# Another order of issue and other places in memory for a four-layer kernel

## The chip, the cores and the metric

The kernel runs on one core of a Trainium2 chip. A core has a matmul engine (TensorE, PE in the profile), a vector engine (VectorE, DVE), an activation engine (ScalarE, ACT), a general one (GpSimd, POOL) and a sync engine (SyncE, SP) that here only issues DMAs. Each engine works off its own queue of instructions in order, and waits at an instruction until what it needs is there. Operands lie in SBUF, an on-chip memory of 128 partitions; products go to PSUM, which has eight banks of 128 x 512 floats here. The metric is the device time of the core in microseconds (us), the median over runs; beside it there is one profiled execution with a record of every instruction.

## The reference: what is computed

Two sequences (batches) of 1024 tokens with 128 channels pass through four layers. Each layer has the same frame, and its own pair of blocks:

```python
xn = layernorm(x)
s = attn_i(xn)
g = silu(ffn_i(xn))
x = x + s * g
```

- Layer 0, attention: q, k and v by projections, causal convolutions of four taps and silu; a delta rule in chunks of 32 tokens with four heads of 32 channels. In each chunk a 32 x 32 triangular system is inverted, row by row; then a state S goes from chunk to chunk:

```python
u_i = ui - wi @ S
o_i = qi @ S + mask(qi @ ki.T) @ u_i
S = S + ki.T @ u_i
```

  Its output is mixed with v and with two longer convolutions of v (7 and 25 taps) by a small router, that takes the input and the means, variances and mean products of the four branches (56 features), has one hidden layer and ends in a softmax. Layer 0, feed-forward: four wide products of 512 hidden channels with gates and gelu, and a narrow one back to 128.
- Layer 1: softmax attention of 16 heads over all 1024 tokens, with a distance-like score; a mixture of eight experts, two for each token.
- Layer 2: linear attention of 16 heads; a block that only the 127 tokens of highest score go through, with attention among these.
- Layer 3: causal attention with 16 query heads and one key head; two blocks of local attention in windows of 64 tokens with rotary positions.

All arithmetic is in 32-bit floats.

## The kernel before

**Two passes.** `program` (L2270) doesn't issue instructions. It runs over layers, batches and blocks and calls the engines through stand-ins (`Engines`, L629), and a `Record` (L493) notes each call as a unit. A unit is one instruction, or on PE a run of up to 32 matmuls of the same shape in the array that follow one another in the same block and batch (`note`, L520; `product`, L548). For each unit it is worked out from the regions of the buffers which earlier units must come first. There are 7120 units. The costs and lags given in the engines' stand-ins are noted, but at issue nothing is decided by them.

**The order** is a table. `ORDER` (L297) is a packed string; `Record.order` (L568) unpacks it into the numbers of all units in the order in which they are issued, with one more bit per unit. A copy out of PSUM that may be done by either of two engines (`evac`, L723) goes to DVE where the bit is set, and else to ACT. There are 480 such copies. Since the blocks of both batches are all in one list, the order also says how they interleave: the recurrence of batch 1 runs among the work of batch 0 for layer 0, and so on.

**The places** are a table too. Tiles come from pools: 35 large ones of 128 x 1048 floats (`half`), 21 of 128 x 512 (`t512`), 14 small ones, eight PSUM banks, and a few more. `PLACES` (L424) gives for each buffer, when its first use is issued, which slot of its pool it takes, 4594 in all. A slot's next buffer can't be written before the last use of the one before.

`Record.issue` (L584) then walks through the order, draws places and issues all instructions from L604; so each row of the profile carries this line, and what an instruction belongs to is read from its operands' names. DMAs are units as well: loads of weights and input are issued by SP, the experts' gathers by POOL.

**Layer 0**, on which much of the following turns, has these steps for each batch (`l0_attn`, L813). The input x is normalised to `xn` (ACT and DVE), transposed on PE (`tr`, with an identity matrix that lies in the first part of `const`) and copied to `xnT`. PE projects it (`proj`, with weights `w_a`), the result is copied to `pad`, and DVE convolves it (`acc`). Norms follow (`ss`), products of keys (`kk`), the triangular systems (`nn`), which go through a scratch memory to another layout (`scr_n`, `ncol`), where a loop of products and sums on DVE inverts them (`prod`, `u`), and back by eight DMAs (`scr_u`, `td`). Then tiny products of 32 x 32 blocks on PE: `pu` (twelve groups of 32, between them copies and subtractions on the way to `uw` and `vk`), `chunk` and `au`, from which DVE makes `step`, `add` and `read`. The recurrence is thirty times the same pair:

```python
C.mm(ps[r, :DH], at(step, c)[r], at(state, c)[r], tile_position=(32 * h, 32 * h))
nc.vector.tensor_tensor(at(state, c + 1), ps[:, :DH], at(add, c), ALU.add)
```

Four matmuls into `next` on PE, one addition into `state` on DVE, each waiting for the other. The convolutions of 7 and 25 taps (`conv`) are 32 DVE instructions over 1024 elements each. Features (`feat`) are transposed to `fT`; the router's hidden layer is `rh`, its output `logit`, its softmax starts with `lg`. The feed-forward block (`l0_ffn`, L1173) has the products `p`, `ph` and `w` on PE (`w` is the narrow one; a group of it is called w3 below), with weights `w_f_0` to `w_f_5`. Layer 1's attention begins with the scores `sim`, then `e` (the exponential on ACT) and `av`.

Of the kernel before, what the change touches and what calls it, by code (L numbers as in the profile page):

```python
# [20 lines left out]
AF = mybir.ActivationFunctionType  # L21
ALU = mybir.AluOpType
X = mybir.AxisListType.X
PSUM = bass.MemoryType.PSUM

P = 128
NB = 2
L = 1024
T = NB * L
NT = T // P  # L30
TB = L // P
# [225 lines left out]
def pack_inputs(inputs):  # L257
# [29 lines left out]
PE, ACT, DVE, POOL, SP = range(5)  # L287
# [10 lines left out]
    "c-mcg2VfLc*Y=#5*^*5sjZ_E;9i(>*L_nJKj#5+<QC@m8o86gBHWX2mA|SkA0TED8I!F^~p$Q@-w2%e~q>!H7o!z<Lxpx+P|9>~xow;+%xu-nm"  # L298
    "Id{K%mk%P9XUU9Vb~SUtly9dFezOLk-u~ACKu`rkT|z-X(3y6m@^L~G|3e>uD1d`Q4i-;`!i!={;aI=hxkDQ69lUNL_TN3|Zy2P9k_!(;HCgd?"
    "<ny26JBL-f{7iM=<JP+XzHoMMkNtTR6n)d`uGOcav}qOa{LXPdz55_KEPsueEStW6UWMN8{{GPkS*_|8uC9g%H+aM%Fg<|wPeUpTIy`;>&{%gD"  # L300
    "60#dVgqTvl2oaZ^wgs-jlO_fI;MHp<1Ppq0b8G;9==O~`r*CK2JEW6AA&npT#PLeunIxql<i;1c60;M&ouBbLe3bz3wc)pM-Qu<xbjudr{J2}d"
    "2=eHkxgWuv7k>IJxl2~0x^-2*zW)LYuDqL5QkzVvGX+!yl=ym_`h@xORB#(eG|c<*ad~(Q{PP+>K`hLl69<J+Wg#d-?yliYEgwh0d*8xiXLGn)"
    "9;{zpZ<=T0SMQ|h;s8Ef4og;Gw;6h6!~Ld_C;JwD^v#4bg%I(4{;DAdBc8t{ck=G2YRs|s_Wa&eyD5pyM^i;ArGqaIuDr<S!Q@>rm3{>gd>06+"
    "46OV$s_SK_D4%)oS6K7C)am1WPovikjeSODH~)Cxi28bmF!blG@1Jq<t4G96Sosn7C{uUTnO4QKsUIwK9D8GPVqaso%fd<lzP(X5we4<c$ib06"
    "6<wG(a`?Vg^IOfF@yi(K^e%ji-B-YmLnDm8z+07jl@AZU`#|vH;PHtMb-s!qE?dO&KB9SHw1Ft5hq0n*>Q-lINrLWSGh#4*RAqE~+^^LY=C^(_"
    "PTd_GeXcRz`<#F3?1-$Y57xpb1CI^*k7E0)<28UmuJc>IA01^)HI{}k>;Hc**#;;3;`jbx07szwV{{mwA3EOUxBBc-q072}wdJn-$Ro68g-ZAX"
    "+n1dY>W$p9a`i{|p=RcH{l~ori4S!z>TQn6I0F?TxPx6T_r)YXSFJz%cgLY&aB7Wy8q@{^uK4cK!7r4f0lnc=pG(0_9ScYNvMA^CMZI7=EH$6r"
    "r8rD4qCQ)dE5zOo+_m5ubST8Qq3-apSv7^u{R*Ji;fa490T6ROZEIj<PCQI~c66%L2<|llV`L8ev)exE@^7C*t|23+#rd89cPe+Rz1sqv0m6l%"
    "F~86q%v$@=E>cks;Ap3z2ZmZYV^d}~rUf4We*4>RZfM*Eek7Ay3k6?I3N1bA@R{-W7}QSRKHPshfN8`}q0OQW_YdAt7&38Ne#hqlRRf>?GvJso"
    ">i7PKl&pmZOCrQd5nnuH&Ddz(0|LPP;&7NH9yl+bc;j@B3jno)Z(Qgx{c7$0x4!w$opa6p=wiZ!HACQ6dzb&^jWYz@u2C1BjXXS9cMRLQ>vSyu"  # L310
    "R&Tp@H1<(kyVW}P>|1vh<ii@Ze8{;uUw40drlA&unb$7}A8wp6rv?Av`cGhe+>pi5dI*>Z8{0!?xZP@76?{Cs?Z=xc7qXRpD{;m^IV||^^J!N*"
    "Ke#je=$pbZo(woVkl)5bQNyobZk;CvDvVX4UsPdDWHtph@Ez51iNBCDYwy$6d9ekBUGgFJ39%0iX<h!#QMlXmZd0d8aR*mG*t7aj?g^_g)v0{T"
    "st54q&k+##La0~k3?xONpu4*OPL+)N^BDw*FAPSVtM5URLm+|WLNFo3DJt=KpeCsKx2{wBPj!?Xf4ew#Uwvq41h-D$d5_L%<ONj`6qCSv+=3CE"
    "67>wV{!S3}YMsBr_snzzD27_yr6iZmr~C(a@4_EtA!RL$<AV9=uy$S3{-iGW(4cjbF7!Vf(Sqy)80HCj;lEUR5@Hh63&&Cg0})k^52-amtVkZ6"
    "nq+Vng$oA7?U$XvD{6IwaxC)fS(rTJdK++=iXucpbSj8~>H#Bh3*xuJqLt&PZxIFe<*pu4AVc6F1Xh2%=|mEU#8eaT&JWJx@Rnk5ebJ_u|Dj}G"
    "hdbC4pUo>iCWq3iiw!-&q?QG!;boqPLSLt->IHBa+=^u`1P0U@Krwi*i>L~8+xR53^p*dxFT;JurVn_xF7UHYmoI|y5WziJ(JMPE;oUtvFOWIw"
    "#JP6k!d-0+EwCHvz~tk^pf!{SK&8P4YJ6M;(E{-SN0eAJ=GUx=H-?{v7reW;c@+`dsQ#P;GWfwmk9q=z#TAGiw_6|gM8AFp@u1EeHCy3lxa4Vj"
    "o97*8d;2?8|KElM&z|S!ERKZunvIWV92@O~pFVl<?E3JA()(nW&xEML+AXo=lU9$ssOuzbSh{LaRX`|Q+45eXP<&xT!L8QUNBA6Xyxy>GNqBYr"
    "*0*;0d^g^MX!1j7am}h_y>2u+Gv?qJfS-4MI(9i9SWQUN(9E_F+vn6_pAU8y^gF?S^GWen?+?BOpC3LQ*Yfw&3tjC7*Vii+%_itN;<}Fo-c%5F"
    "bK0A7i(k9Pk6+}5`O#amvd7eB1($R1ciX?)1U3A7!p{}Sov*BJy>6{DSa^5qUtEX4-@;qpU%Jn8EwSI#7kwZpcI23!biOP8S(no+2R>gDb1M72"  # L320
    "KRRC9lyRCrJ|H>d-Iz2|Ij=#bW3hUr^V$_9K1T-=P*rE*lx@YKe97#^ZJrB@KNrt-zu4UqQc<rwI43qQp~}aI!Jrq_^3Y0OLtR9tAgA#;c)$QP"
    "5Vw8OkNqJCj`DfY@wug9^Be7Sx4@%wd#Xd*hMw%Fh$CT8LwBbeuZ5rMpLgk6pT>{)H;#*Zx!(8LU;UF8PtA>Qc0V`n(7+Qz;c-3qI%OGv`9Z?+"
    "rg6}E)glqr&2g?UFO}L4H?Ntq6wJypSn4qG<XXEWymWV$U0GdeldWJ{vT_k`^+~V$Y_VOq>h9q%iF21__E@~qz&mtvR&AMP0A2w-U*ihUdBk_W"
    "uMMg7==@ZNfp@ue#v0M%8`*jIKJHZ(ax~Z3m*~<0${G|zLai^)lPA#FLHz2ToS2>s8#7X~_GdMAY?~6i^22v_cygf~%eVKyF*@lue3-KAj+C~o"
    "fA4_;5dtcLNo5f5Rl(){4pSxeGU*&XzIBB6D+^V4QWpfzLaSaE&ihoo4(AbgLZBsF@*(wweE$W?x5f3<O1{pdl)elreEBJ1B_7!MRo<6V129#L"
    "?Ai;uor8ugclWP-QBP3o-+_9f!$)-bT<i{>BNIgxj<z@W9}ySAdH3%FK^4LTC<-eHE8YKE!foVZ7oNiiFjo5W^<MDgR#JJO)91Gl6{mN7>(U9z"
    "!I51Tj}|&ya@QV&$+ueZ;O2#MNxbn`GI1LeW8$L*c@4H2x_Jx$p1n`fUO0RMx58Y=&1&XZo;YUJl*Gm2&u_0=Qvr{+*6Oo^EA%%H#>RHMW*lBr"
    "9V%G66;8b}=qUJzoy!N#8!KLj{a%Q@*b}0RPU9afgJUoBKGPOAkvV_#I|+535870GkiVflxz%?eT+Z!UH1GSr8pc7x*k}<NJ+^;dk(|4BX3m03"
    "FK!>4xTaxjVw}IQanGss^EbSGd+j%Y`3LeIZ1eo{T1M3PT^)Q|JHRI$W&zav)TN!_613%}yiqs$_LbC2@o!E0U}?WL8Fwr$bH#oq9KHR{iYY@J"
    "74<EdEn1chSik08y#9XEmHA+Xz?}6BVR2F9O$hofsCL#Ps6IX`aK&3NY0}s|ec{&f22qLI8!RP}3$O1B^5egLZ>Ft2{PIWZ83k{jb$0^4v+d*Z"  # L330
    "|H^B9tG+(aeqx(Xm-@$s^i55;1f%oesxT5B>n}{+M`{9&t?haS3NCepe}?U-3n@z`X9j1!_BRiv+e0A`&a@5szF}JsZWXr)`hD=ph&v6%@?N%;"
    "-K;^L$02^BbvK~xUET5SOZ$cub?@`lJG+FpVoSmrTuTr2gHmIcTdi-6^7*k<r)A6Dn2>O*>a^u%RrP15JhzPlzOl=_T3`Ls$GWyj2e>lu*nKFR"
    "SA4Q>GsCKd$Nz>lJ&wWy0UEve4NN~@D^HnN8+q(;qk*2Yj*dTcxSh}uxz-1RM||SsPZ*)c$-Ylb{SUeBJ{kZYo;cS0;M=3kJx}#{TIqjiz{BV!"
    "uz5(m^PR6Zf^5ugx?2xNJ<vyHZJ6EWXJO#&M~N+cuD$UmG<bBcnFzN%)3?ImCG}4<T05^Be`f9CX)t@xf~C*kpEE0#%=~Jp!83P2ygz)lrr(+X"
    "n7Zzp!Z4kCG0ZRNUNrmrIk2%tuOB-*)Vg(kd2o4PLXXR?*VleO^}pr22kswsr1LuY@{!J=jY4fgtLR4U^J*N~2_cbl6W)39<Fd_nrk%bty2bC8"
    "S7&dp*Q62}Gz44snO6gDwLadYYRq51wCGq_S^m6Xa6Q=8JvV>!(^#KR-)s|7{ZDoGi}&AB5_3Fvd~06|ygJ~>{g4L1&DMW%vDBykt<ds<qKd>?"
    "MHIS*?(AOgwap379hJ|Ux4Q8FIzIhqc}qui4%CZMdS1TS&ebBv@8B9pi}JZ?&)YJ1cnPd7Y&CXu+2f%_4;wvRFAr`rH$1HLEBR_d=Udn2!`jW;"
    "9z5>cpdkF<qWy`jPX}i<;U7ibHP!bk4vsAl2QL^)?p6ffiZAln2Xim#Eo#=|ORM1T`2L#?)&2O+kC5SZExoa`Lrc+~(tJw0d(({%AN4%sd#YP$"
    "K<CEJl&(*LrtnR!?eQJs+|YPX-QnEu$(_fUrrf`=5GI|w2ZkzRS(nS-zwdU`^R>m+-RnHS6HwLK5m6jfS01d(+%fYTcL3ix%-5;gavu2AM~3g6"
    "28P_kGRs<UW=H!>hV_DAh%9+A?r_HEi?8gfF@C%Wk`F}BUF55)Do;$Sm4u{|RVIDvjG#cGyczo9)R^+B*B<N(SaQDSYIpLFn^u;8>R-L8t-+Uf"  # L340
    "clfd{B{MU%_p+^nMoJ5TEHmG3k;xyp-ffx7w4^T05`1yV@j=}|QpG-pWW(XU_Kb_IKK~RPpXWSZmhx`BK0wZN`eau2ZP_+A&^5IC;?I^r`HJi_"
    "C2GW@#?Na6S5TSWQ(rNb2XE_DFKp6xkKWzuTR5r7+WA}Z-|qV`?flwpA8Zza^h0WntM!sR{iQmcuBg+AofBHZ?ST1B9&Deq%N=cj^k-09lzyk!"
    "vNZP|z=WNn>tNo-x`T4kS-B;z#Qx>q^~DmBQC#`K{>n)^`IwTrQJ_23XUF(^1!De$U6!21(Cpq$o6$4;po*+1pb^|C4JGZG-QV7N&y*wm-@0`5"
    "`CB<{Z=QMQ$br6HNDHIu_n4hi{`}N9^NUmV{-UevKxKKS=Jkz7q1lyx(#hUMw+?12->us>;!5Yf_x3N!FRowI>d)A^DnDHiWX0YZ{GxE-Mx@bx"
    "H5HM$ysq(GdrJQk&5hy3j<{SQt7%kLppoQ8J>gpvKWOWl9a!1)Nv&UKUbrErQU5KG<sDB8eALtTH%-lJlGSw68%;JFqlDT<PYpu*or&!)-uZAx"
    "bZMLdYI5C`#yNaW{N;XsCj|OM@^I&$wvBhYJCw$UU+t0AJg5D&&ii9(O2aQrtbexqUqa%Y=65`;0^0v~`j#QWj#)=8cIQFO8@c9_15@El&MbK3"
    "15pQB317yI2e{M@_RKli=<nPw@KN%glefILcJ_9)+*j{zakt&A1QIF4?d)+@H(tHgd7H6z>eVbkZQlL64lnXY3(lJzu6NwgPN)jMpu7?1`fOB-"
    "v)ytU=hn2m3%W#CHs6dq)SbNc&4gv;pVdUJAGI>?=Z)Ek(<^EY-d+58Zts~T?NT1k)3rAbgD!lX@dn>C>Xbpzm-|h=ShOKMi{JiX<NWaYaJh+x"
    "ztoY`JDa4x+$7u8^kIjr)@o)8Da|E>mM(X#J=s2J&Z@<b_F^eNuKDteo6T)Up?Q!}SFhTqI@nRA7hC~QB?vxWPYA8$_wX@K>-Q$cABz^O@r}8;"
    "Xi-G1&nKDC_4?fer}6LhIY!<OjIaMT;?k4y%D_h{8@gYucztEc<419o6%9<!e((36+6fEJ82Cn8x@9I2&*d)u)w(dJGkSX;!k=uX4-m?`>#qI&"  # L350
    "+vcPFYDh0yjJedCN=0&;ht3=BsgJ>x*{>|@P_swA-41oq`6>a2`J|foUmLf{{=0+!pWVonK?jHI?Q*gAS-zj&@y=(HziVjdp<GDzWcEB?2OS$d"
    "HJ&o{s=ewAbw3IpwqNXdv8SK9I62vL__XZ}Pjdg26O4mTuDDn+ZjRu#d(zC1C3HRA$^Pl>11XjXU5``^vc4J6CR6CKZ_Fu=`g#EHWoP-J$GQZZ"
    "IAFh6GAvT45sG?bC*EtazH8`#p(WwPzAZ|_ub)Y3d+&FC!Y<eFMz>uT2mdx<m)JWp;J<g9>H&J4trMKa-lxXx=Lf60lC!GF3*92x@WcT(_01uD"
    ";!l=rcoc8waJgXwe>LXH(2{#TZC|KIhk=q``)K%`CghR6fnGcr*7~+@19x^~-zq<o<7O9!Nf8|YS6gRwQ_pucsh0}I*5769oY@0@O|HBhbbe;z"
# [2024 lines left out]
```

## Time and profile before

| | |
|---|---|
| median of three runs | 1859.08 us (1857.2 to 1860.61) |
| the profiled execution, as timed | 1849.79 us |
| its span, first to last instruction | 1848.0 us |
| PE busy | 1705.1 us, 92% |
| DVE busy | 1319.8 us, 71% |
| ACT busy | 1075.4 us, 58% |
| POOL busy | 444.4 us, 24% |
| mean granted TensorE clock | 0.951 |
| first product of layer 1's scores (`sim`) | 455.5 us |

Busy time is the time in which an engine executes something; what an engine waits for is listed beside an idle stretch, with the engine and tile that ended it. The clock is the share of TensorE's full speed that was granted. In timelines a row has the start, the duration, the engine, the line, the operation, out<-in, the count of instructions put together in that row, and in brackets the idle time before it and what ended that. In rows of waits there are the total in us, the times and the longest.

### The profile page before, as it was taken

The numbers are of one execution on the slowest core, as the hardware profiler recorded it, in microseconds if no ns is written. First come the engines' busy times: TensorE is split into PE (matmuls) and PEld (weight loads), VectorE is DVE, ScalarE is ACT, GpSimd is POOL, SyncE is SP. The second block draws the span as 40 slices with busy tenths as digits, with TensorE's granted clock in tenths as the row PEclk, the third lists the DMA queues.
The fourth block names the chain that finished last, engine by engine and source line by source line (L and its number), as shares of the span: only waits on it lengthen the run. The fifth ranks groups of instructions, "written<-read, shape, count | busy, mean of one in ns | idle before, by whom it ended". The sixth has DMA issues, their size and how long they took to land.

```text
span 1848.0 us, 37236 instructions
## 1 busy us (share of the span) xinstructions
PE 1705.1 (92%) x15060; PEld 996.9 (54%) x15060; DVE 1319.8 (71%) x2769; ACT 1075.4 (58%) x1999; POOL 444.4 (24%) x448
## 2 busy tenths in 40 slices
PE   6985998677999999999999999999998999999997
PEld 3464454555333863248465478654356666544485
DVE  6956888578113555425799998988986888877865
ACT  4211434124988578973646566665756777665653
POOL 0001120212231343332311461223303611530000
PEclk9995889777999999999999999999999999999999
DMA  3000011000132232235140122102001210001021
GB/s 122 13 14 9 1 19 39 15 14 3 42 94 80 92 111 68 79 103 155 44 127 13 48 75 65 36 1 60 1 29 47 85 37 25 1 1 43 7 74 35
DMA packets 68300, 88.97 MB, mean 48 GB/s; under 512 B 29568, under 2 KB 41856, under 8 KB 68000
## 3 DMA queue, kind: packets, MB, share of 16 engines
q1 hardware_dynamic: 59008, 57.26, 10.9%
q0 software_dynamic: 9120, 29.33, 5.5%
q8 instruction: 118, 1.93, 0.5%
q14 instruction: 54, 0.44, 0.1%
HBM read 79.62 MB, written 6.95 MB: 47 GB/s over the span
## 4 chain that ended last, share of the span: by engine, by line
PE 43%; DVE 10%; ACT 2%; DMA 2%; issue 2%; SPq 1%; POOL 0%; DVEq 0%; ACTq 0%; POOLq 0%
PE sim L604 11%; PE num L604 8%; PE wo L604 3%; PE tr L604 2%; PE down L604 2%; PE av L604 2%; DVE u L604 2%; PE z L604 2%; PE q L604 1%; SPq L604 1%; PE qk L604 1%; PE up L604 1%; PE a L604 1%; DVE qf L604 1%; PE g L604 1%
## 5 line engine op out<-in xcount | busy, mean ns | idle before, releaser
L604 ACT ACTIVATE e<-sim 128x512 f32<-128x512 f32 (+3 forms) x896 | 427.2, 565 | 145.7 <-PE sim L604 69.8
L604 PE MATMUL num<-e,v 128*64 128x512 f32 (+4 forms) x1280 | 181.8, 424 | 0.9 <-ACT e L604 0.8
L604 DVE TENSOR_TENSOR e<-e 128x512 f32<-128x512 f32 (+3 forms) x320 | 168.4, 562 | 14.9 <-ACT e L604 6.9
L604 POOL TENSOR_TENSOR sq<-qk,tab 128x256 f32<-128x256 f32 x128 | 106.8, 855 | 224.7 <-DVE ss L604 141.8
L604 PE MATMUL sim<-q,k 32*128 32x512 f32 x1024 | 155.0, 644 | 3.8 <-DVE q L604 3.4
L604 PE MATMUL sim<-q,kT 64*128 64x512 f32 (+3 forms) x768 | 144.0, 504 | 1.8 <-ACT e L604 1.8
L604 ACT ACT_TABLE_LOAD x98 | 125.7, 1283 | 16.8 <-DVE k L604 10.5
L604 PE MATMUL av<-e,va 128*32 128x512 f32 x1024 | 134.8, 606 | 0.0
L604 PEld LDWEIGHTS num<-e,v 128*64 128x64 f32 x1280 | 82.6, 137 | 87.9 <-issue 69.5
L604 PE MATMUL ph<-h,w_f 128*128 128x512 f32 x256 | 114.2, 603 | 3.9 <-ACT h L604 2.5
L604 PEld LDWEIGHTS sim<-q,kT 64*128 64x128 f32 x768 | 71.1, 188 | 79.2 <-ACT e L604 36.0
L604 PEld LDWEIGHTS sim<-q,k 32*128 32x128 f32 x1024 | 49.1, 185 | 95.8 <-ACT e L604 72.4
L604 POOL TENSOR_TENSOR u<-u,sq 128x512 f32<-128x512 f32 x64 | 89.0, 1401 | 1.7
L604 ACT ACTIVATE e<-e 128x320 f32<-128x320 f32 (+3 forms) x160 | 76.1, 527 | 22.6 <-DVE e L604 21.7
L604 DVE TENSOR_TENSOR sim<-sim,const 128x128 f32<-128x128 f32 x256 | 65.5, 292 | 31.4 <-PE sim L604 28.2
L604 PEld LDWEIGHTS ph<-h,w_f 128*128 128x128 f32 x256 | 48.7, 193 | 63.5 <-issue 57.3
L604 DVE SCALAR_TENSOR_TENSOR conv<-vT,w_a,conv 128x1024 f32<-128x1024 f32 x60 | 80.8, 1350 | 0.8
L604 POOL DMA_INDIRECT xg<-xd,index x46 | 46.2, 1005 | 123.9 <-DVE index L604 80.1
L604 POOL DMA_INDIRECT we<-in_experts,index x46 | 43.7, 950 | 131.3 <-DVE index L604 45.6
L604 DVE SCALAR_TENSOR_TENSOR e<-sim,const 128x320 f32<-128x320 f32 (+2 forms) x128 | 60.7, 529 | 11.8 <-PE sim L604 10.5
L604 PE MATMUL qk<-w_f,shifted 128*128 128x512 f32 x128 | 64.6, 630 | 4.6 <-ACT sq L604 4.4
L604 DVE TENSOR_REDUCE ss<-sq 128x8 f32<-128x512 f32 x96 | 62.8, 674 | 1.8 <-ACT sq L604 1.6
(545 smaller groups left out, 3489.5 us busy)
## 6 DMA issues: line engine op xcount, KB each, us to landing
zb<-zd SPq DMA_DIRECT2D x192, 128.0 KB
tab<-in_rotary SPq DMA_DIRECT2D x8, 512.0 KB
yd<-y SPq DMA_DIRECT2D x10, 256.0 KB
w_f<-in_f SPq DMA_DIRECT2D x4, 512.0 KB
mk<-in_mask SPq DMA_DIRECT2D x4, 512.0 KB
w_l<-in_l SPq DMA_DIRECT2D x4, 512.0 KB
w_f<-in_f SPq DMA_DIRECT2D x4, 448.0 KB
const<-in_const SPq DMA_DIRECT2D x1, 1041.5 KB
```

The lines of the kernel that those rows point to most:

```text
L604: tc.keep_in_program_order(f(*map(real, args), **{k: real(v) for k, v in kw.items()}))
```

## The change

Both tables are replaced, and nothing else: the code that reads them is the same, as are the units and what must come before what. The new order table takes one line of source more, so instructions are issued from L605 instead of L604.

```diff
 ORDER = (
-    "c-mcg2VfLc*Y=#5*^*5sjZ_E;9i(>*L_nJKj#5+<QC@m8o86gBHWX2mA|SkA0TED8I!F^~p$Q@-w2%e~q>!H7o!z<Lxpx+P|9>~xow;+%xu-nm"
...
+    "c-mcA2UrwW*Pb(F3mrrh8;Tt@C>AWSfxT<&8WT;_L}N=dF)X_?yDTOe^Vwq5s8JI?d+)s~_FiJJi;75xUD%zSng857tKakd$ivRwx#iqb-t(Sg"
...
 PLACES = (
-    "c-keHiF(^OuZ97VASrQ?D9WyroNROd7x}-;=`(FJw!{VaHdOwT-=FWVPx(Ljcz=8Sdp_E&DrrV_7QCd}MR%FbE7al5hv9-t8vUv6uz0SYyM^TQ"
...
+    "c-kG8*>>Z)4nzTh1P6&4C?$3h=jJ5;|B-jI`ys1sQxt|mRYCrK<v;oP-}me5^W)idedxWszsW86at$L`OqXOIYB8K9=i%{)Dtp*B&z8Cd^<Zm="
...
```

Unpacked, the tables say this. Half of the 7120 units stand within 16 places of where they stood, nine in ten within 70. Of the 480 copies that either engine may do, ACT has 349 before and 337 after, DVE 131 and 143. The number of places in ACT's queue at which another function table has to be loaded falls from 95 to 91. The order of the first ten loads on SP's queue is

```
before: x (batch 0), w_f_1, w_f_0, x (batch 1), const, w_f_2, w_f_4, w_a, w_f_5, w_f_3
after:  w_f_1, w_f_2, x (batch 0), x (batch 1), w_f_4, w_f_0, w_a, w_f_3, const, w_f_5
```

In layer 0 of batch 0 one group of the feed-forward's narrow product, `w`, which stands before the first `pu` group in the old order, stands behind the fourth in the new; two groups of `au` that stand ahead of the first `next` stand behind it; and the transpositions of batch 1's `xn`, which follow batch 0's recurrence in the old order, stand within it in the new. Such moves are found in all layers.

## The prediction

> **What bounds the kernel now.** I read the page first (busy shares, slices, chain), then a table of windows of 46.2 us (a fortieth of the span), PE's waits, and the timelines where a wait stood out.
>
> ```profile
> PE 1705.1 (92%) x15060; PEld 996.9 (54%) x15060; DVE 1319.8 (71%) x2769; ACT 1075.4 (58%) x1999; POOL 444.4 (24%) x448
> ...
> PE   6985998677999999999999999999998999999997
> ...
> DVE  6956888578113555425799998988986888877865
> ...
> PEclk9995889777999999999999999999999999999999
> ...
> PE 43%; DVE 10%; ACT 2%; DMA 2%; issue 2%; SPq 1%; POOL 0%; DVEq 0%; ACTq 0%; POOLq 0%
> ```
>
> The matmul engine is the bound: busy 92%, idle 1848.0 - 1705.1 = 143 us. The digits say where: from the eleventh slice on, PE stands at 9 almost throughout; the first ten hold 6, 8, 5, 6, 7, 7, and there the clock digit falls as well. The windows (columns: stretch; its length; busy time and instructions of PE, weight loads, DVE, ACT, POOL; clock; DMA share; GB/s):
>
> ```profile
> 92.00:138.00 46.00, 38.54 (x1020) 28.31 (x1018) 27.13 (x40) 7.95 (x13) 1.48 (x8) 0.97 0.09 14
> 138.00:184.00 46.00, 24.85 (x1136) 20.08 (x1137) 28.52 (x89) 7.33 (x11) 7.37 (x4) 0.50 0.03 9
> 184.00:230.00 46.00, 41.95 (x118) 19.00 (x117) 39.80 (x43) 19.91 (x29) 8.11 (x5) 0.82 0.00 1
> ...
> 323.00:369.00 46.00, 30.06 (x1200) 26.54 (x1188) 24.06 (x58) 8.81 (x15) 12.14 (x15) 0.76 0.06 15
> ...
> 508.00:554.00 46.00, 46.00 (x359) 14.18 (x356) 7.60 (x24) 41.32 (x82) 16.35 (x16) 1.00 0.32 92
> ```
>
> Over the ten windows up to 462 us (layer 0 of both batches, delta-rule attention with its recurrence of thirty steps) PE's busy times add to 368.6 us, so 93 of the 143 idle us lie there; 50 are spread over the 1386 us behind. The same ten windows' clocks show about 154 us at half speed. So layer 0 is bound by chains PE - DVE - PE, the rest by PE's throughput. The waits of PE agree (total us, times, longest):
>
> ```profile
> PE next L604 <- DVE state L604: 19.5, 42, 1.1
> PE tr L604 <- DVE xn L604: 14.3, 4, 12.2
> PE pu L604 <- issue: 9.9, 7, 2.1
> PE au L604 <- issue: 7.1, 4, 2.0
> PE chunk L604 <- issue: 7.1, 6, 2.1
> ```
>
> The recurrence (next on PE, state on DVE), the start (12.2 us until xn is there), and gaps in which PE waits for nothing the profile shows, among thousands of tiny 32x32 products.
>
> **What the Trainium skill says.** "TensorE: Matmul & The Clock Gate", section "What's actually happening": an idle window of some 3.4 us halves the clock, a busy one restores it. The trace agrees: 0.50 in 138-184, where PE is busy 54%. "DMA: Bandwidth & Descriptors", section "Issuing engines are not separate DMA queues": issuing more queues adds no bandwidth; in the trace, SP's ten first loads are issued by 6.7 us and their packets run one load after the other at some 200 KB per 0.5 us until 17.4 us. "Runtime: NRT & Kernel Launch", section "Instruction fetch mechanics": fetching is mostly hidden; the trace disagrees where passes are tiny, with an issue gap of 1.5 to 2 us about every 128 of them. "ScalarE: Activation LUTs", section "What ACT_TABLE_LOAD costs": 1283 ns, as in the page's 98 loads.
>
> **The change, part by part.** The same 7120 units of work are issued, in another order, and 4594 buffers get other places. I laid both lists beside the trace, gave each unit the duration measured for it before, and summed each engine's queue ahead of landmarks.
>
> *No work is saved.* Twelve copies out of PSUM go from ACT to DVE (about 0.68 us there, 0.60 on ACT: DVE +8, ACT -7 of busy time, hidden on both after 462 us, where DVE is below PE). Table switches in the list fall from 95 to 91: 4 x 1.283 = 5.1 us of ACT, hidden by PE. Half of the units move under 16 places. PE's 1705 us stay, so a gain can only come out of the 143 idle us and the half clock.
>
> *The start, +3.9 us.* Now:
>
> ```profile
> 0.74 0.44 SPq L604 DMA_DIRECT2D x<-in_x  x1
> ...
> 2.79 1.10 SPq L604 DMA_DIRECT2D const<-in_const  x1
> ...
> 12.18 1.95 PE L604 MATMUL tr<-const,xn 128*128 128x128 f32 x8 [12.18 <-DVE xn L604]
> 16.05 1.19 PE L604 MATMUL proj<-xnT,w_a 128*128 128x512 f32 x1 [1.91 <-DMA w_a<-in_a]
> ```
>
> Before, x is the first load and const (1041.5 KB, with the identity that every transposition reads) the fifth. After, two weight loads stand ahead of x and const is ninth of ten. By the packets' pace, const lands at about 17.1 us; x two loads later, 1.9 us, so xn at 14.1 is covered. The first transposition goes from 12.18 to 17.2, the first proj from 16.05 (where it waited for w_a) to about 20.0: +3.9. This start is nearly bare on PE; DVE's first acc, which waits for proj's copy, gives back part of it (+2.2), as ACT takes the xnT copies and the pads. Bounds: +2 to +5.
>
> *Up to the recurrence of batch 0, -1.5 us.* From 16 to 113 us PE is continuously busy, so its queue carries the delay. DVE's work ahead of the first nn falls 43.9 to 36.0 us, ahead of the first prod 69.6 to 54.9, ahead of td 94.4 to 84.1: td, which the first pu needs, is earlier for DVE and is not the limit. One w3 group (3.4 us) moves from before the first pu to between pu groups: first pu at +3.9 - 3.4 = +0.5; by the first next it is there again. Two au groups and some tr and rh (2.5 us) move behind the first next, and of tiny passes ahead of it there are 1024 for 1152, one issue gap less (1.7) while the w3 covers most of another (1.2). First next: +3.9 - 2.5 - 2.9 = -1.5 (bounds +4 and -5).
>
> *Recurrence.* 145 to 179 us, thirty steps of about 1.1 us; the hand-offs stay: 0. The eight transpositions of batch 1's xn (1.5 us at that clock) move from behind it into its pauses: -1.5 for batch 1's proj.
>
> *Batch 1's first half, -5.*
>
> ```profile
> 204.44 0.60 PE L604 MATMUL tr<-const,feat 128*56 128x128 f32 x4 [1.03 <-DVE feat L604]
> 207.32 2.05 PE L604 MATMUL rh<-xnT,w_a 128*112 128x512 f32 x2 [2.29 <-DVE fT L604]
> ...
> 234.39 0.29 DVE L604 TENSOR_TENSOR lg<-logit,w_a 128x128 f32<-128x128 f32 x1 [6.97 <-PE logit L604]
> ```
>
> PE waits here 1.03 + 2.29 = 3.3 us for DVE, and the clock is at half from 207 to 221, 13.7 us, of which up to 6.9 are lost. After, DVE has 153.5 us ahead of the last feat for 160.5, and 157 ahead of fT for 163 to 173; PE reaches the transpositions 6 us later in its queue (143 for 137). So DVE is about 10 us better placed: the 3.3 us go, and I take a quarter of the clock's loss: -5 (bounds 0 and -10). DVE's own wait of 6.97 at the logits shrinks too (169 ahead for 181). In batch 1 itself step has 261.7 for 269.8 and the last state 297.1 for 301.5 of DVE work; of that I take 1 us, as PE's queue there is unchanged (first sim of layer 1: 295 for 293). First sim: -1.5 - 1.5 - 5 - 1 = -9 (+-6).
>
> *After it, +2.* PE-bound; what remains is how closely results stand to their uses. Counting PE units whose nearest foreign result is issued less than its own duration plus the hand-off (0.04 to 0.06 us in the trace) ahead, I find 113 before and 137 after, with shortfalls of 108 and 123 us in sum. The trace turned the 108 into some 50 us of idle, so 15 more are worth up to +7; against that stand fewer switches and a better placed ACT in layer 1 (ACT units with too little ahead 132 to 113). I take +2, bounds -5 and +9. POOL's gathers and SP's weight loads keep their distance to within some us of PE work; some gathers of batch 0 stand close, but others did before and no gap of PE named them.
>
> Sum: 1848.0 - 9 + 2 = 1841. The profiled execution (1849.79, of which 1848.0 span) is 9.3 under the median of the runs, 1859.08; by the same step the median is **1852**.
>
> **Rivals.** *A, slower: the delayed start passes through.* const at the ninth place costs 3.9, the w3 put among pu groups 3.4 more on the way to the recurrence. For it: PE has no gap from 16 to 113 in which to make up a delay. Against it: 2.5 us of au, tr and rh stand behind next now, and DVE is earlier everywhere. It decides if first next comes later than +4 and the waits at feat come back elsewhere: 3.9 + 3.4 = +7, **1866**. *B, given back:* layer 0 gains 5 to 9 us, and after 462 us the tighter hand-offs (137 for 113) take 7: **1859**. A change that isn't what it says falls under this: by my count the distance between result and use hasn't grown for PE. *C, more:* the 154 us of half clock shrink. If the 207-221 stretch (6.9) and half of those at 369-462 (clock 0.71 to 0.72, some 26 us each at half, 13 lost each) are run at full speed, about -20 in all: **1839**. For it: DVE is 4 to 12 us ahead at every landmark; against: the recurrences, 34 and 50 us of half clock, are as they were.
>
> **How the numbers follow.** My forecast (-3.7 to -15) 0.45; C 0.16; B (within 0.2%, 3.7 us, about what a measurement of this kernel tells from no change) 0.14; A 0.18, and 0.07 for a transfer or an ACT chain after 462 us that goes wrong by more than 10. Faster 0.61, same 0.14, slower 0.25. The likeliest alone: 1844 to 1855. Range for 8 in 10: C's far half (to 1836) and A with some above (1869).
>
> **What would show it.** Right: first transposition at about 17 us, first proj at 20; first pu near 113.7 (now 113.2); first next at 142 to 145 (now 145.25); no feat or fT wait over 1 us and a clock above 0.82 in 184-230; first sim of layer 1 some 9 us before the 455.5 of now; idle of PE after it still near 50. Wrong: first next after 149, layer-0 waits that only change their names, or idle after the first sim that grows by over 8 us.

## The result, and the profile after

The changed kernel takes 1832.62 us (median of four runs, 1830.15 to 1836.64), the kernel before 1859.84 (four runs, 1857.2 to 1863.41): ratio 0.9854, 95% interval 0.983 to 0.9879, 27.2 us less. The prediction had the direction, and missed the size: 7 us, range 1836 to 1869. The two profiled executions differ by less: 1836.64 us after (span 1834.8), 1849.79 before (span 1848.0), 13.2 us. In the five batches of experiments that followed, on four chips, the kernel before has medians from 1844.1 to 1847.7 us over 219 runs; 164 of these lie between 1836 and 1851, and a fifth (43) between 1853 and 1865, with twelve between the two. The 43 are called the upper group below, though no clear gap sets them off; all four runs of the first comparison lie in its range.

The page after: busy line, slices of PE and clock, chain.

```profile
PE 1690.3 (92%) x15060; PEld 986.0 (54%) x15060; DVE 1327.8 (72%) x2781; ACT 1066.8 (58%) x1984; POOL 437.6 (24%) x448
...
PE   6985999677999999999899999999999999899997
...
PEclk9995989678999999999899999999999999999999
...
PE 76%; DVE 15%; issue 4%; ACT 2%; DMA 2%; POOL 1%; SPq 0%; DVEq 0%; ACTq 0%; POOLq 0%
```

DVE has 8.0 us more, as the prediction has it, and ACT 8.6 less; the twelve copies and four table loads of the prediction come to 12 there, and 95 loads are left of 98. PE's idle time is 1834.8 - 1690.3 = 144.5 us for 142.9: the 13 us did not come out of idle time, but out of PE's busy time, 14.8 less with the same 15060 matmuls. PE at half clock counts as busy in the profile. By the clock records and PE's rows, 129.5 us of its busy time before lie at half clock and 118.7 after; work that passes from half to full clock takes about half the time (a run of rh below 3.75 us for 1.97), so these 10.8 us are worth 5.4 of the 14.8. Where the other 9 come from is not shown. The windows of layer 0 (columns as before):

```profile
92.00:138.00 46.00, 37.85 (x895) 26.62 (x894) 30.48 (x32) 8.59 (x14) 3.55 (x5) 1.00 0.15 31
138.00:184.00 46.00, 25.37 (x1262) 20.64 (x1262) 24.46 (x76) 9.33 (x13) 5.01 (x6) 0.52 0.01 4
184.00:230.00 46.00, 45.28 (x146) 24.58 (x147) 43.81 (x54) 25.87 (x39) 8.05 (x3) 0.91 0.00 1
...
323.00:369.00 46.00, 29.80 (x1271) 26.08 (x1271) 27.25 (x75) 7.11 (x10) 14.22 (x19) 0.66 0.05 15
```

From 184 to 230 us PE is busy 45.28 for 41.95 and DVE 43.81 for 39.80, at a clock of 0.91 for 0.82. In the windows of the recurrences (138-184, 323-369) PE's busy time is within 0.6 us of what it was, 25.37 for 24.85 and 29.80 for 30.06. PE's waits up to 462 us, and its start:

```profile
PE next L605 <- DVE state L605: 22.5, 38, 3.0
PE tr L605 <- DMA const<-in_const: 16.9, 1, 16.9
PE pu L605 <- issue: 11.3, 9, 2.2
PE chunk L605 <- issue: 9.0, 5, 2.3
PE tr L605 <- DVE cmp L605: 8.7, 1, 8.7
```

```profile
16.93 1.94 PE L605 MATMUL tr<-const,xn 128*128 128x128 f32 x8 [16.93 <-DMA const<-in_const]
18.69 4.55 PE L605 MATMUL proj<-xnT,w_a 128*128 128x512 f32 x8
```

The late const ends the wait of 16.9 us, where xn ended one of 12.2. Layer 1's first scores, before and after:

```profile
446.40 2.09 PE L604 MATMUL sim<-q,k 32*128 32x512 f32 x8 [2.91 <-DVE q L604]
```

```profile
437.76 1.14 PE L605 MATMUL sim<-q,k 32*128 32x512 f32 x8 [0.55 <-DVE q L605]
```

They begin at 446.40 us before, and not at 455.5, which the table of the time before and the prediction give: a later run of sim begins there, behind layer 0's last product. First to first it is 8.6 us. To see where time goes, I took the first start or last end of named tiles in each trace, and the length of the stretches between them (us; half: time at half clock in it; idle: PE idle in it). "Again" is a second profiled execution of each, from the first batch below.

| stretch, up to | before: length, half, idle | before again | after | after again |
|---|---|---|---|---|
| first pu, batch 0 | 113.2, 3, 15 | 113.2, 3, 15 | 113.9, 3, 20 | 114.2, 3, 20 |
| first next, batch 0 | 32.0, 10, 11 | 29.8, 8, 9 | 30.5, 5, 10 | 28.7, 3, 8 |
| last state, batch 0 | 34.2, 34, 17 | 32.9, 33, 16 | 39.1, 39, 18 | 38.9, 39, 18 |
| last u, batch 1 | 118.9, 31, 9 | 117.4, 28, 9 | 107.0, 25, 4 | 106.3, 23, 3 |
| first next, batch 1 | 48.1, 7, 9 | 47.7, 7, 8 | 43.5, 7, 8 | 42.4, 7, 7 |
| last state, batch 1 | 38.2, 31, 19 | 36.9, 34, 16 | 38.6, 28, 15 | 38.5, 27, 15 |
| last product of layer 0 | 71.0, 38, 15 | 71.0, 38, 15 | 73.1, 34, 20 | 73.1, 34, 20 |
| the end | 1392.4, 26, 50 | 1389.7, 17, 49 | 1389.0, 36, 50 | 1385.1, 31, 48 |

Up to the end of layer 0 the changed kernel is ahead by 9.8 us in the first pair (6.7 in the second), at the end by 13.2 (11.3). Between the two lies more: where layer 1's last product ends (down, from the experts), it is ahead by 17.6 us (15.7), 848.9 for 866.5, with 8822 and 8833 of the matmuls done. So some 8 to 9 us are gained in layer 1 as well, and 4.4 us lost again behind it.

### The profile page after: what moved, and what is told of

Read it like the earlier page. It is cut to its first block, busy times and chain, and to the rows that moved or that the text cites. A ratio compares the mean times of both kernels' runs of the same rounds, so it can differ in the third digit from the quotient of the medians.

```text
span 1834.8 us, 37233 instructions
## 1 busy us (share of the span) xinstructions
PE 1690.3 (92%) x15060; PEld 986.0 (54%) x15060; DVE 1327.8 (72%) x2781; ACT 1066.8 (58%) x1984; POOL 437.6 (24%) x448
## 4 chain that ended last, share of the span: by engine, by line
PE 76%; DVE 15%; issue 4%; ACT 2%; DMA 2%; POOL 1%; SPq 0%; DVEq 0%; ACTq 0%; POOLq 0%
PE sim L605 16%; PE num L605 8%; PE ph L605 6%; PE av L605 6%; PE tr L605 5%; PE down L605 3%; PE wo L605 3%; PE up L605 2%; PE qk L605 2%; PE z L605 2%; DVE u L605 2%; DVE e L605 2%; PE p L605 2%; PE q L605 1%; PE pu L605 1%
## 5 line engine op out<-in xcount | busy, mean ns | idle before, releaser
L605 ACT ACTIVATE e<-sim 128x512 f32<-128x512 f32 (+3 forms) x896 | 427.7, 562 | 144.9 <-DVE sim L605 70.2
L605 PE MATMUL num<-e,v 128*64 128x192 f32 (+4 forms) x1280 | 184.1, 426 | 4.3 <-ACT e L605 4.3
L605 DVE TENSOR_TENSOR e<-e 128x512 f32<-128x512 f32 (+3 forms) x320 | 175.2, 583 | 10.8 <-PE num L605 5.5
L605 POOL TENSOR_TENSOR sq<-qk,tab 128x256 f32<-128x256 f32 x128 | 103.5, 830 | 235.7 <-DVE ss L605 165.4
L605 PE MATMUL sim<-q,kT 64*128 64x512 f32 (+3 forms) x768 | 148.9, 511 | 2.5 <-ACT e L605 2.4
L605 PE MATMUL sim<-q,k 32*128 32x512 f32 x1024 | 149.5, 637 | 1.5 <-DVE index L605 0.9
L605 PE MATMUL av<-e,va 128*32 128x512 f32 x1024 | 135.1, 606 | 0.0
L605 PEld LDWEIGHTS num<-e,v 128*64 128x64 f32 x1280 | 82.5, 138 | 94.9 <-issue 73.8
L605 PE MATMUL ph<-h,w_f 128*128 128x512 f32 x256 | 120.0, 624 | 0.7 <-DVE ko L605 0.7
L605 PEld LDWEIGHTS sim<-q,kT 64*128 64x128 f32 x768 | 71.2, 189 | 82.3 <-ACT e L605 34.5
L605 PEld LDWEIGHTS sim<-q,k 32*128 32x128 f32 x1024 | 44.3, 183 | 94.7 <-ACT e L605 65.5
L605 POOL TENSOR_TENSOR u<-u,sq 128x512 f32<-128x512 f32 x64 | 90.8, 1429 | 1.6
L605 DVE TENSOR_TENSOR sim<-sim,const 128x128 f32<-128x128 f32 x256 | 64.6, 291 | 36.4 <-PE sim L605 35.6
L605 ACT ACTIVATE e<-e 128x320 f32<-128x320 f32 (+3 forms) x160 | 76.3, 527 | 16.0 <-DVE e L605 13.9
L605 PEld LDWEIGHTS ph<-h,w_f 128*128 128x128 f32 x256 | 50.0, 201 | 59.7 <-issue 57.6
L605 DVE SCALAR_TENSOR_TENSOR conv<-vT,w_a,conv 128x1024 f32<-128x1024 f32 x60 | 77.8, 1306 | 1.0
L605 POOL DMA_INDIRECT we<-in_experts,index x46 | 43.3, 942 | 129.8 <-PE sim L605 34.1
L605 POOL DMA_INDIRECT xg<-xd,index x46 | 44.4, 964 | 123.5 <-DVE index L605 67.0
L605 PE MATMUL qk<-w_f,shifted 128*128 128x512 f32 x128 | 63.0, 617 | 5.4 <-DVE u L605 3.5
L605 DVE SCALAR_TENSOR_TENSOR e<-sim,const 128x320 f32<-128x320 f32 (+2 forms) x128 | 62.5, 529 | 7.4 <-PE sim L605 7.0
L605 ACT ACTIVATE h<-ph,w_f 128x512 f32<-128x512 f32 x32 | 21.5, 687 | 78.5 <-PE ph L605 78.4
```

What stands on the lines that cost most here:

```text
L605: tc.keep_in_program_order(f(*map(real, args), **{k: real(v) for k, v in kw.items()}))
```

## The experiments

Both tables are packed, so edits were made to the unpacked lists, and packed again. A unit keeps its engine unless the text says otherwise. Where two orders are joined, places come from each order's own table, its slots renamed where the other part still holds them.

**First: both kernels again, and the two orders joined after layer 0.** In r1_before_again and r1_after_again nothing is edited. The joined order takes the first 1202 units from one list, the rest as they follow in the other:

```diff
-order = old
+order = new[:1202] + [u for u in old if u not in new[:1202]]   # r1_l0_after
+order = old[:1202] + [u for u in new if u not in old[:1202]]   # r1_l0_before
```

> The kernel before, unchanged, in another profiled execution. Theory 1 (the profiled execution of before, 1849.79, was a lucky one; a usual one holds about 9 us more, and these are part of what the change removes): the new profiled execution lies within 4 us of the median, 1855 to 1863, and against the old one the difference of 6 to 13 us sits in one or two places, with more half clock there (the ten windows to 462 us hold over 160 us at half speed, for 154). Rival (the profile costs nothing and the scatter is spread): any time from 1850 to 1863, with the end of layer 0 within 2 us of 455.6 and the rest spread over the stages behind it.

> The changed kernel, unchanged, in another profiled execution. Theory 1: 1828 to 1837 as in its four runs; end of layer 0 near 446, within 4 us, so the changed kernel scatters less than the one before. Rival: its scatter is as wide as that of before (some 13 us from the lowest to the highest), so that part of the 27 us between the medians is chance.

> The first 1202 units in the new order with the new places (all of layer 0 but its last 20 units, and 230 units of later blocks that stand among them), the rest in the old order and the old places, up to a renaming of slots. Theory A (the gain is made in layer 0): within 4 us of the changed kernel, 1829 to 1837. Theory B (it is split as in the two profiles, 10 of 13 us up to the end of layer 0): 1836 to 1842. Theory C (half of it is made later): 1843 to 1850.

> The counterpart: the first 1202 units in the old order and places, the rest in the new. Theory A: 1855 to 1862. Theory B: 1850 to 1855. Theory C: 1842 to 1849. The gains of this kernel and its counterpart should add to the whole, 27 us, if the two parts don't work on one another.

Measured: before again 1846.47 us (1840.26 to 1859.22), against 1847.72 for the runs of the kernel before in this batch; its profiled execution 1840.26. So the first theory fell: it is not the profiled execution of before that was low, it is the first median that was high. After again: 1831.62 (1828.78 to 1838.4), ratio 0.9906 (0.9874 to 0.9938), 16 us. r1_l0_after 1853.08 (ratio 1.002, 1.0003 to 1.0037) and r1_l0_before 1857.00 (1.0045, 1.0022 to 1.0067): both slower than either kernel, which no theory had of the pair; that 1857.00 lies in theory A's range says little, as this range was laid round the 1859.84 and the kernel before has 1847.72 in this batch. In r1_l0_after layer 0 is as in the changed kernel (first sim of layer 1 at 437.8 us, as there), and the loss comes at 590 to 650 us, in a view of PE's waits:

```profile
PE up L582 <- DMA we<-in_experts,index: 7.0, 2, 4.5
PE up L582 <- DVE h L582: 2.3, 2, 1.4
```

At that cut seven units around the experts' gathers had to be put off until a slot for their indices was free, and PE stood waiting for the experts' weights. This pair tells what a late gather costs, not where the gain is made.

**Second: single parts, and a cut without such a seam.** r2_after_start puts SP's first ten loads back into the old order; r2_after_lru keeps the new order and draws places by a plain rule; r2_l01_after and r2_l01_before cut at unit 2760, behind nearly all of layers 0 and 1, where nothing has to be put off.

```diff
-w_f_1, w_f_2, x0, x1, w_f_4, w_f_0, w_a, w_f_3, const, w_f_5
+x0, w_f_1, w_f_0, x1, const, w_f_2, w_f_4, w_a, w_f_5, w_f_3   # r2_after_start
-place = next(PLACES)
+place = the free slot whose last use is longest ago            # r2_after_lru
```

> The changed kernel with one part undone: the first ten loads on SP's queue stand in the old order again (x first, const fifth). Theory (the late const lies on the path, step 1 of the prediction): the first transposition goes from 16.9 back to about 12.2 us, the first proj from 18.7 to 16.0, the first pu from 114 to about 111, and the time falls by 2 to 4 us, to about 1828 where the changed kernel has 1832. Rival (the later steps wait for something else anyway): the first pu stays within 1 us of 114, the time within 1 us of 1832.

> The new order of issue, with places drawn by a plain rule (of the free slots of the pool the one whose last use is longest ago) instead of the new table. Theory (the order makes the gain, places matter little): 1829 to 1838. Rival (the searched places are a part of the gain): 1842 or more, with waits of PE, DVE or DMAs at the first writes of buffers.

> The first 2760 units in the new order and places (layers 0 and 1 but 94 of their units, and 150 units of layer 2), the rest in the old order and places up to a renaming of slots. No gather's unit has to be put off at this cut, as seven were at the cut of r1_l0_after, where PE then waited 7 us for experts' weights. Theory A (the gain is made in layer 0, the loss of that kernel was the cut's): 1829 to 1838. Theory B (the two orders are each tuned as a whole, every seam costs some 10 us): 1843 to 1853. Theory C (a third is made behind layer 1): 1836 to 1842.

> The counterpart: the first 2760 units old, the rest new. Theory A: 1845 to 1852, as the kernel before has 1848 on this chip. Theory B: 1855 or more. Theory C: 1840 to 1845. The slower executions, 1855 and over, which the kernel before shows in a fifth of its runs, stay with this kernel if they come from layer 0, and are gone if they come from the layers behind.

Measured, with 1844.13 us for the kernel before: r2_after_start 1827.46 (0.9904, 0.9877 to 0.9931), its first pu at 111.5 for 114.2 us. So the late const costs 2.7 us up to there, and the time is where its theory had it, 4 us under the 1831.62. But the 1831.62 come from another chip, on which the kernel before was slower too, by 3.6 us; against the kernel before the ratios are alike (0.9904 and 0.9906), so what is left at the end is not settled. r2_l01_after 1829.18 (0.9917, 0.989 to 0.9944), r2_l01_before 1847.63 (1.003, 1.001 to 1.005), with single executions up to 1859.9: theory A. The whole gain is made by the order and places of layers 0 and 1; the new order of the layers behind is no better than the old one and, put behind the old front, slightly slower. From the end of layer 1 to the end of the kernel, r2_l01_after, with the old order there, takes 980.3 us, the changed kernel 985.9 and 982.9. r2_after_lru, 1851.20 (1.0026, 1.0007 to 1.0044), is the miss of this batch: places drawn by the rule cost 20 us. Up to the first pu its profile is 9.3 us behind the second one of the changed kernel, most of it by one wait:

```profile
PE ph L583 <- DVE ka L583: 8.1, 1, 8.1
```

The product ph reads nothing of ka; a copy into ka empties a PSUM bank after a transposition, so what ph waits for is, by this, a bank. Up to the end of layer 0 it is 13 us behind; another 6 us go in layer 1, and the rest of the 25 between the two profiles behind it. The prediction had not priced the places at all.

**Third: where within layer 0, the copies, and a version meant to beat both.** r3_l0a_after cuts at unit 840, about where batch 1's recurrence begins. r3_after_copies gives each of the 480 copies the engine it had before. r3_best2 is r2_l01_after with x, const and w_a first on SP's queue. r3_best2_fill adds to it, ahead of each recurrence step, a product of the identity with itself into columns of the bank that nobody reads:

```diff
         ps = C.bank("next")
+        C.mm(ps[:, 128:256], C.ident, C.ident)                 # r3_best2_fill
         for h in range(H):
```

> Only the first 840 units in the new order and places (up to the last pu groups of batch 1, some 330 us; nearly all of them layer 0), the rest old. Theory A (the gain is made before batch 1's recurrence, by the work of batch 1 that now stands within batch 0's): first next of batch 1 near 331 us as in the changed kernel (341 in the kernel before) and most of the gain stays: 1830 to 1836. Rival (the old order behind it gives it back: recurrence and router of batch 1 wait for others): 1838 to 1846.

> The new order and places, but each of the 480 copies out of PSUM on the engine that it had before: 194 of them change sides, 12 more are on ACT again. Theory (the engine matters little on its own, the prediction put it at nothing): 1829 to 1836. Rival (order and engines belong together, the copies come late on the busier engine): 1840 or more, with PE waiting for copies in layer 0.

> A version meant to beat both: the first 2760 units in the new order, the rest in the old (as in r2_l01_after, 1829), and the first ten loads put so that x of batch 0, const and the projection's weights come first, in this order. Theory (start and middle add): the first transposition at about 12.2 us and the first proj right behind it, near 14, for 18.5; if the 4 us carry through as in r2_after_start, 1823 to 1826. Rival (PE was waiting for DVE after the start anyway): 1827 to 1830.

> The same, with one useless product of 128x128 into unused columns of the bank ahead of each of the 60 recurrence steps, so that PE is busier there. It tells what the half clock in the recurrences costs. Theory C of the prediction (the half clock is a cost of its own): the clock over the two recurrences rises from 0.50 and 0.64 to over 0.8, the two recurrences shorten by some us each, and the time falls below that of r3_best2 by 3 to 10 us. Rival (a step is bound by the hand-offs between PE and DVE, and by the small products' issue): the clock may rise, but the time stays or grows by the 60 products of 0.2 to 0.4 us, up to 12 to 24 us if none fits into a pause.

Measured, with 1844.28 us for the kernel before: r3_best2 1822.91 us (1822.16 to 1825.96), ratio 0.9866 (0.9825 to 0.9908). It is faster than the kernel before, and all six runs lie under the lowest of the changed kernel's ten (1828.78), which come from another batch. Its start:

```profile
12.26 1.97 PE L582 MATMUL tr<-const,xn 128*128 128x128 f32 x8 [12.26 <-DVE xn L582]
14.05 5.89 PE L582 MATMUL proj<-xnT,w_a 128*128 128x512 f32 x8
```

r3_after_copies 1863.20 (1.0089, 1.0063 to 1.0115), the largest miss of the study. Of the 480 copies 194 are on the other engine; the twelve of the prediction are only the balance. Back on the old engines they cost some 30 us. In the profiles (29 us apart) it is spread: 3 up to the end of layer 0, 6 in layer 1, 3 and 5 in the stretches to the ends of layer 2 and of batch 0's layer 3, 12 behind, with no one wait that names it. So the new order needs its own engines for the copies; the old order with the new engines was not run.

In r3_best2_fill PE is much busier in the recurrences, and the clock does not follow. The windows 138-184 and 323-369 of r3_best2, then of r3_best2_fill:

```profile
138.00:184.00 46.00, 28.22 (x1097) 20.77 (x1084) 29.31 (x85) 9.98 (x15) 7.15 (x7) 0.52 0.01 4
...
323.00:369.00 46.00, 30.19 (x1206) 25.53 (x1205) 30.98 (x80) 5.58 (x10) 14.57 (x18) 0.64 0.05 15
```

```profile
138.00:184.00 46.00, 41.34 (x1077) 31.17 (x1076) 23.82 (x72) 8.17 (x9) 4.75 (x6) 0.54 0.01 3
...
323.00:369.00 46.00, 42.44 (x1093) 34.91 (x1092) 23.79 (x67) 7.11 (x10) 10.08 (x16) 0.65 0.05 15
```

PE is busy 90 and 92%, the clock 0.54 and 0.65, and the time 1836.85, 14 us more. The two recurrences take 44.5 us for 38.8 and 46.0 for 38.3 in the profiles, which is nearly all of that. What the half clock in them costs stays open, as the fill didn't lift it.

r3_l0a_after 1842.48 (0.9961, 0.9941 to 0.9981) lies between the two theories, and its 22 runs fall into two parts: six from 1830.2 to 1834.0, where the first theory has them, and sixteen from 1838.6 to 1849.9. Its profiled execution has the first next of batch 1 at 333.7 us and the last state at 369.2, as in the changed kernel (369.1), and loses 10.7 us between there and the end of layer 0: 83.8 us for 73.1, with 63 us at half clock for 34. r1_l0_before, whose first 1202 units are those of the kernel before, shows the same, 84.4 and 57; r2_l01_before, with the same units there, 71.5 and 37. The same products on PE in r1_l0_before,

```profile
405.26 2.08 PE L583 MATMUL tr<-const,feat 128*56 128x128 f32 x8 [3.85 <-DVE cmp L583]
...
416.97 3.75 PE L583 MATMUL rh<-fT,w_a 56*112 56x512 f32 x4
...
422.03 3.78 PE L583 MATMUL rh<-fT,w_a 56*128 56x512 f32 x4
...
428.25 3.96 PE L583 MATMUL logit<-w_a,rh 128*128 128x16 f32 x33
```

and in r2_l01_before:

```profile
397.26 2.09 PE L582 MATMUL tr<-const,feat 128*56 128x128 f32 x8 [3.96 <-DVE cmp L582]
...
405.18 1.97 PE L582 MATMUL rh<-fT,w_a 56*112 56x512 f32 x4
...
407.84 1.98 PE L582 MATMUL rh<-fT,w_a 56*128 56x512 f32 x4
...
411.09 4.16 PE L582 MATMUL logit<-w_a,rh 128*128 128x16 f32 x34
```

After the same wait of 3.9 us the router's products take 23.0 us to the logits in one and 13.8 in the other. In the first, PE has no pause from 405 to 428 us and still stays at half clock: in the two windows from 409 to 429 it is busy 10.00 of 10 us each, at a clock of 0.50 and 0.54. In r3_l0a_after PE is busy from 389 to 419 us at 0.50. So the upper part of that kernel's runs is this stretch at half clock, as far as its one profile shows; r1_l0_before's profile (1872.85) is the highest of its runs.

The traces show something more. In all twenty profiles the clock changes only at whole steps of 3.41 us, and where these steps lie differs from execution to execution. Eight profiles have the old order in this stretch. In six of them the transpositions behind the wait start 2.1 to 3.3 us after such a step, and the clock is back at full after one step at half; their waits are 2.3 us in four and 4.0 in two. The two that stay at half start 0.9 us (r1_l0_before) and 1.5 us (r3_l0a_after) after one, behind waits of 3.9 and 4.2 us.

**Fourth: is it so in the kernel before?** Three more profiles of it, unedited, and the counterpart of r3_l0a_after: the first 870 units old, the rest new.

> The kernel before, for another profile. Theory (its scatter comes from the stretch behind batch 1's recurrence): over all its profiles, the time less the length of this stretch (71.0 us in two profiles so far) varies by less than 6 us; an execution over 1853 shows 80 to 86 us there, with 55 to 63 us of half clock for 37. Rival (the scatter is spread over many places): a slow execution shows less than 75 us there.

> The same kernel and the same two theories, with one more profile: a slow execution is seen in about one of four.

> The same kernel and the same two theories, with one more profile.

> The first 870 units in the old order (up to batch 1's first recurrence steps), the rest in the new. Theory: the executions over 1853 are gone, lowest to highest within 10 us as in the changed kernel, and the median lies some 2 to 6 us under that of the kernel before, 1838 to 1843, as the 10 us made ahead of batch 1's recurrence are lost. Rival: the scatter stays as wide as before (over 15 us), the median within 3 us of the kernel before.

Measured: the three kernels have three, none and three of their ten runs over 1853 us, but all three profiled executions (spans 1843.5, 1845.4, 1840.1) fell into the lower group, with 71.0, 71.5 and 71.0 us in the stretch. So an upper execution of the kernel before itself was not caught in a profile; that it looks like r1_l0_before and r3_l0a_after is inferred. r4_l0a_before: 1845.90 (0.9995, 0.9978 to 1.0011), 14 runs from 1839.6 to 1847.6, none in the upper group, as its theory had it. That is not much: with 11 of 73 runs of the kernel before in that group in this batch, 14 runs without one come by chance about once in ten times. The median is 3 us above what the theory had, and where the rival had it.

**Fifth: what in the order does it.** In the new order two router products over all 128 rows (rh from xnT) stand right behind the wait, ahead of those over 56 rows (rh from fT). In the old one they stand ahead of the wait. r5_before_dense moves two of them in the old order; r5_after_thin does the reverse in the new.

```diff
 # r5_before_dense, PE's units around the wait, old order
-rh(xnT)  wk  rh(xnT)  wq | tr tr wv rh(fT) ...
+wk  wq | tr tr wv rh(xnT) rh(xnT) rh(fT) ...
 # r5_after_thin, new order
-tr tr wv rh(xnT) wk rh(xnT) rh(fT) rh(fT) ...
+tr tr wv rh(fT) rh(fT) wk rh(xnT) rh(xnT) ...
```

> The kernel before with two of PE's 7120 units moved: two products of the router's hidden layer over 128 rows (rh from xnT), which stood ahead of the wait for the features (tr waits for cmp), now stand behind it, after wv and ahead of the products over 56 rows (rh from fT), as two of them do in the new order. Theory D (products over all rows right behind the pause bring the clock back, those over 56 rows don't): no executions more than 8 us above the lowest half of its runs, where the kernel before has 3 of 10; the median 1842 to 1846, as the wait itself grows by the 2 us moved behind it. Rival E (the clock's state there is set by the phase of its windows and by the length of the pause): the upper group stays, a sixth of the runs or more over 1853.

> The changed kernel with three of PE's units moved in the same stretch: wk and two rh from xnT (128 rows), which stood right behind the wait and wv, now stand behind the first two rh from fT (56 rows). Theory D: an upper group appears, some runs 8 us or more above the lowest half, as in the kernel before. Rival E: 1828 to 1838 as before, within 10 us.

Measured: r5_before_dense 22 runs from 1839.34 to 1850.07, none over 1853, where the kernel before has 7 of 40 over 1853 in the same batch; median 1845.14 for 1845.17. Its wait is 4.8 us for 2.3 to 4.0 in the five profiles of the kernel before, as the two moved products had filled part of it, and the stretch 74.4 us for 71.0 in the profile. r5_after_thin: 19 runs from 1825.77 to 1843.91; twelve up to 1832.1, and seven from 1834.7 up, four of these over 1838.4, which is the highest of the changed kernel's ten runs. Both results are as theory D has them, but neither is proof. Chance gives none of 22 beside 7 of 40 about once in 26 times, and four of 19 beside none of ten once in six. Neither profile (1848.03 and 1831.96 us) caught an execution that stays at half clock there. And the edit of r5_before_dense also lengthens the wait, which rival E counts as a cause. In its favour: the profile of r5_before_dense resumes 1.5 us after a step of the clock, as r3_l0a_after does, and is at half clock for two steps, where r3_l0a_after stays for eleven. That the place of the pause among the steps matters (a part of rival E) is what the eight profiles above suggest; that the order matters beside it rests on this pair and on the counts of runs.

## Why the prediction was wrong

The sum at the end of layer 0, -9, measured -9.8 us in the profiled execution (-6.7 in the second pair; first sim, against its true start, -8.6). That it fits is in part luck: two of its steps were off by 5 us and more, and cancelled.

- *The start, +3.9:* the first transposition was forecast for 17.2 us and came at 16.93; proj came at 18.69, not 20.0, as it starts behind the first copy of xnT (18.05, 0.59 us on ACT). +2.6 at proj; undone, it is worth 2.7 us at the first pu.
- *First pu, +0.5:* +0.7. *First next, -1.5:* -0.9.
- *Recurrence of batch 0, 0:* wrong, +5. Its steps were put at unchanged hand-offs, but work of batch 1 now stands among them on both engines, and it is 39 us for 34. *Batch 1's proj -1.5 and first half -5:* what moved in is missing behind: 118.9 to 107.0, -12. The sum of the three, -6.5, measured -7. No wait for fT or feat over 1 us is left, and the clock at 184-230 rose from 0.82 to 0.91, as said, but not by a DVE that is 10 us better placed: it has 178.5 us of work ahead of the first lg (169 forecast, 181.0 before), and the transpositions of feat start at 208.21 us for 204.44. PE comes later, with more work of its own ahead, and both copies of fT are on ACT.
- *Batch 1's later steps, -1:* -4.6 up to the first next, then +0.4 and +2.1 behind it: -2.
- *After layer 0, +2:* -3.4 in this pair, -4.6 in the second, as the sum of two parts: about -8 in layer 1 (-9 in the second pair) and +4.4 behind it. PE's idle time over both is unchanged, 49 to 50 us, so the tighter hand-offs that I counted don't show as idle time. What makes layer 1 shorter at the same idle time I did not settle.
- *The copies at nothing:* right only for the twelve of the balance, and wrong as a reading of the change: 194 change sides, and with the old sides the new order loses 30 us. *The places:* not priced; 20 us hang on them.
- *The half clock:* the prediction takes 0.50 at 138-184 as agreeing with what it cites of an idle window of 3.4 us. In that window no gap of PE is longer than 2.4 us, so the trace shows half clock on a PE that is busy 54%, and no idle window.

The step that failed is the last: "by the same step the median is 1852". It took the 9.3 us between the profiled execution and the median as a fixed distance. For the changed kernel the profiled execution is 4.0 us over the median of its runs, so that the step is off by 13.3 of the 19.4 us between 1852 and 1832.62; the other 6.2 are the sum up to it (7 for 13.2), 5.4 of them in the term behind layer 0, +2 for -3.4. Put otherwise, 27.2 = 13.15 (profile to profile) + 10.05 (the profile of before under its median of now) + 4.02. The 10.05 are no constant: in the later batches the medians of the kernel before lie at 1844 to 1848 us, and its profiled executions on both sides of them. Measured side by side in one batch (1847.72 and 1831.62), the change is worth 16 us; with the other batches' medians it would be 12 to 14. The rest comes with the first median of the kernel before, whose four runs all lie in the range of the upper group, where a fifth of the later runs do. Why all four do is not explained; a slower chip, or another cause that acts on that comparison alone, is not ruled out.

Rival A (the late start passes through) had the start's cost right and its end wrong. Rival B didn't come about. Rival C, 1839, is nearest in time and partly in mechanism: half clock does matter, but not where it was put. The stretch that decides is behind batch 1's recurrence, not at 207 to 221, and there the change, as far as runs and profiles tell, makes half clock rarer rather than shorter.

## What to carry to other kernels

A profile is one execution: before a median is derived from it, look at how the runs scatter, and where they form groups, ask of each group which stretch makes it. Where PE pauses for some us on a chain of another engine, try its fullest products first behind the pause, and those over few rows later: here 22 runs with that edit show none of the executions that are 10 to 15 us longer, though the median did not move. An order of issue, the engine of each copy and the places of buffers are one table: the new order with the old copies' engines, or with places by a plain rule, lost 20 to 30 us, more than the 16 us that the whole set gains in one batch. Load first what the first instruction of the bounding engine reads.

## What the hardware showed that I had not expected

- PE that is busy without a pause can stay at half clock: from 405 to 428 us in r1_l0_before, and at 90% busy through a whole recurrence (0.54) in r3_best2_fill, whose filling products had an identity as both operands. How busy PE is in the profile does not tell its clock. This departs from what the Trainium skill states in "TensorE: Matmul & The Clock Gate", section "What's actually happening", that a busy window of some 3.4 us restores full speed: the first of these stretches is 23 us long.
- The steps of the clock lie differently in each execution, and this moves the time. Five executions of the kernel before, r4_l0a_before and r5_before_dense reach the first pu at 113.0 to 113.6 us; r1_l0_before and r2_l01_before, which begin with the same units, reach it at 117.3 and 117.2, with PE as busy. The first rise of the clock on record comes at 18.9 to 20.2 us in the seven, and at 22.1 and 22.0 in the two; then the seven are at half clock for one step, near 40 us, and the two for two steps, from 46 to 53 us, where sixteen ph products take 10.1 and 10.2 us for 7.1.
